# Layer 3 of a four-layer image network: the depthwise convolution of image b done by VectorE, and both engines' instruction orders written by hand

## The chip, the cores and the metric

The kernel runs on one core of a Trainium2 chip. The metric is the device time of one execution, in microseconds (us). A core has several engines that run side by side, each with its own queue of instructions taken in order: TensorE (PE) multiplies matrices and writes only to PSUM, the accumulator memory; VectorE (DVE) does elementwise work; ScalarE (ACT) does copies and functions such as Gelu; GpSimd (POOL) does small elementwise work; SyncE (SP) issues transfers between the core's working memory (SBUF) and the device memory. Engines wait for one another through semaphores.

## The reference

The input x is 4 images of 48 channels and 256 x 256 pixels, fp32. Four layers follow, each of the form x = x + f(normalised x), where the normalisation is over 16 groups of channels. Layer 0 is a gated convolution block, layers 1 and 2 are scans over rows and columns, and layer 3, which the change is about, is this:

```
y  = einsum(w_in, x)                    # 48 -> 288 channels
f  = rfft2(8x8 patches of y) * mask     # a weight per channel and frequency
y  = irfft2(f)
y  = depthwise 3x3 convolution(y, w_dw) # each channel with its own nine taps
x1, x2 = halves of y                    # 144 channels each
out = einsum(w_out, gelu(x1) * x2)      # 144 -> 48 channels
```

## The kernel before, in words

**Steps.** Layer 3 (`layer3`, from L707) takes the images two at a time: image a and image b of a pair. A pair is worked through in 32 steps of 8 rows and a short last step, so there are 66 steps, 64 of them full. A convolution needs one row above and below, so each step keeps ten rows and copies two of them from the step before.

**Tiles of a step.** Of the 288 channels of an image, 144 are x1 and 144 are x2. The first 128 of x1 are one tile, the first 128 of x2 another: a0 and a1 for image a, b0 and b1 for image b. The remaining 16 + 16 channels of both images share a fifth tile, m, of 64 partitions.

**Pieces.** Each step is prepared by pieces of TensorE work, each with its evacuation: `normed` (ScalarE normalises the fetched rows into u), `turned` (TensorE transposes u, 16 columns of pixels at a time; ScalarE copies), `waves` (the forward transform of the patches, into xf), `spectrum` (per column of 8 x 16 pixels the product with w_in into PSUM, L841, and the mask multiplied onto it by VectorE into z, L843 and L847), `pixels` (the inverse transform of one of the five tiles, L872, copied by ScalarE, L876, into the tile zt; GpSimd copies the two old rows, L865).

**The convolution.** `taps` (L883) does it on TensorE: one tap of a channel is a product with a diagonal matrix. It uses 32 x 32 tiles of the array; two *lanes* of work, lane 0 on the partitions 0 to 63 and lane 1 on 64 to 127, each put one tap at a time, 8 matmuls of 512 pixels, into the order. Lane by lane the sums of the first and second half are gathered in PSUM; `gate` (L896) takes Gelu of the first on ScalarE (L903) and multiplies it with the second on VectorE (L904). The layer has four PSUM buffers of two banks each, which is all of PSUM, and every piece and every running sum takes one.

**The store.** `mixed` (L906) multiplies the gated channels with w_out (L917): 32 partitions at a time, image a into the PSUM partitions 0 to 63 and image b into 64 to 127. It takes two PSUM buffers. VectorE adds the layer's input (L930), SyncE stores.

**The order.** `in_turns` (L427) writes TensorE's order by hand: in each round both lanes put one tap each if they can, a tap earns `pace` of credit, and pieces are put in as long as there is credit for their charge. A piece can have a condition (the last user of its tile is through); a lane waits until its tile is ready. The list of pieces is `work` (L965). Only TensorE's order is fixed (L721); the instructions of VectorE, ScalarE, GpSimd and SyncE are ordered by the framework's planner, which goes by its own costs. PSUM and SBUF buffers are handed out by the planner too. Layer 0 uses the same `in_turns`.

Of the kernel before, what the change touches and what calls it, by code (L numbers as in the profile page):

```python
# [15 lines left out]
C = 48  # L16
# [3 lines left out]
PW = 16  # L20
# [8 lines left out]
class Net:  # L29
# [396 lines left out]

    def in_turns(self, lanes, pieces, pace):  # L427


        piece, credit, count = next(pieces), 0.0, 0  # L430
        while lanes or piece:
            moved = 0
            for k, l in enumerate(list(lanes)):
                if k == 1 and count < 4:
                    continue
                got = next(l, None)
                if got is None:
                    lanes.remove(l)
                moved += bool(got)
            count += moved > 0  # L440
            credit = min(credit + pace * moved, 2.0)
            while piece and piece[0]() and (credit >= 0 or not moved):
                piece[2]()
                credit, moved = credit - piece[1], 1
                piece = next(pieces, None)
            assert moved or not lanes

# [259 lines left out]
    def layer3(self, x, scs):  # L707
# [9 lines left out]
        with ExitStack() as st:  # L717
            pool = lambda name, bufs, **k: st.enter_context(tc.tile_pool(name=name, bufs=bufs, **k))
            wp, io, mid = pool("w3", 1), pool("io3", 2), pool("mid3", 1)
            ps_w = pool("ps3w", 4, space=PSUM)  # L720
            st.enter_context(tc.manual_schedule(engines={mybir.EngineType.PE}))  # L721

# [25 lines left out]
            for k in range(3):  # L748
                for t in range(9):
                    nc.vector.tensor_scalar(diag[:, k, t, :], eye, wd[:, k, t : t + 1], None, ALU.mult)  # L750


            wo = wp.tile([128, 6, 64], F32, name="wo")
            nc.gpsimd.memset(wo, 0.0)
            for j in range(4):
                s = slice(32 * j, 32 * j + 32)
                nc.sync.dma_start(
                    wo[s, 0:4, 0:C], self.a["L3_w_out"][0:NM, :].rearrange("(k c) o -> c k o", c=32)
                )
                for b in range(2):  # L760
                    at = 32 * j + NR * b
                    nc.sync.dma_start(wo[at : at + NR, 4 + b, 0:C], self.a["L3_w_out"][NM:HD, :])
# [13 lines left out]
            for p in range(self.NP):  # L776
# [4 lines left out]
                scp.append(t)  # L781
            gated = {g: wp.tile([128, 4, MM], F32, name=f"g_{g}", tag=f"g_{g}") for g in "ab"}
            gated["m"] = wp.tile([128, 1, MM], F32, name="g_m", tag="g_m")
# [15 lines left out]
            def normed(step):  # L799
                raw, sc = raw_of[step], scp[step[0]]  # L800
                u = mid.tile([112, NQ, 2, RB, PW // 2], F32, name="u")
                for e in range(2):
                    for l in range(2):
                        nc.scalar.activation(
                            u[:, l::2, e].rearrange("p v h w -> p v (h w)"),
                            raw[0:112, e, :, :, l * 8 : l * 8 + 8].rearrange("p (v f) h w -> p v (f h) w", f=2),
                            AF.Identity, bias=sc[0:112, 1:2], scale=sc[0:112, 0:1],
                        )
                return u
# [15 lines left out]
            def waves(xt):  # L825
                xf = mid.tile([112, NQ, 128], F32, name="xf")
                for q0 in range(0, NQ, 8):
                    pf = ps_w.tile([128, 8, 128], F32, name="pf", tag="w")
                    for q in range(8):
                        nc.tensor.matmul(pf[0:112, q, :], xt[:, q0 + q, :], self.dft_p, start=True, stop=True)  # L830
                    nc.scalar.copy(xf[:, q0 : q0 + 8, :], pf[0:112])
                return xf
# [63 lines left out]
            def gate(step, img, k0, x1, x2):  # L896
# [7 lines left out]
                nc.vector.tensor_tensor(to[0:n, k0:k1, 0:m], gl[0:n, 0 : k1 - k0, 0:m], flat(x2), ALU.mult)  # L904

            def mixed(step):  # L906

                p, s = step
                h0 = s * RB - 1
                js, n = (range(1), 1) if tail(step) else (range(4), R2)  # L910
                pos = [ps_w.tile([128, 2, R2, W], F32, name="po", tag="w") for _ in js[::2]]
                for i in range(5):
                    for j in js:
                        for b in range(2):
                            r = slice(32 * j, 32 * j + 32)
                            src = gated["m"][r, 0] if i == 4 else gated["ab"[b]][r, i]
                            nc.tensor.matmul(  # L917
                                pos[j // 2][64 * b : 64 * b + 64, j % 2, 0:n, :], wo[r, i + b * (i == 4), :],
                                src[:, 0 : n * W].rearrange("p (r w) -> p r w", w=W),
                                start=(i == 0), stop=(i == 4),  # L920
                            )
# [24 lines left out]
            def lane(l):  # L946

                for n, step in enumerate(steps):
                    for img in ("a", "b") + (("m",) if step[1] % 2 == l else ()):
                        pds = []  # L950
# [14 lines left out]
            def work():  # L965
# [3 lines left out]
                def back(step, k):  # L969
# [5 lines left out]

                    free = lambda: last not in steps or k == 4 or taken.get((last, order[k]), 0) == 2
                    return free, 0.0 if tail(step) else 3.8, go

# [6 lines left out]
                def front(step):  # L985
                    yield always, 1.8, lambda: state.update(xt=turned(state["u"]))
                    yield always, 3.8, lambda: state.update(xf=waves(state["xt"]))

                def spectra():
                    for q in range(0, NQ, 2):  # L990
                        yield always, 1.2, both(*[lambda q=q + i: spectrum(state["xf"], q) for i in range(2)])

                def store(step):
                    full = lambda: all(taken.get((step, g), 0) == (1 if g == "m" else 2) for g in order)

# [3 lines left out]

                    return full, 4.5, go  # L1000

                fetch(steps[0])
                state["u"] = normed(steps[0])
                yield from front(steps[0])
                yield from spectra()
                fetch(steps[1])
                yield back(steps[0], 0)
                yield back(steps[0], 1)
                for n, step in enumerate(steps):
                    nxt = steps[n + 1] if n + 1 < len(steps) else None  # L1010
                    ahead = nxt is not None and not tail(nxt)
                    later = steps[n + 2] if n + 2 < len(steps) else None
                    if ahead:
                        state["u"] = normed(nxt)
                    yield back(step, 2)
                    if n:
                        yield store(steps[n - 1])
                    if later is not None and not tail(later):
                        fetch(later)
                    yield back(step, 3)  # L1020
                    if ahead:
                        yield from front(nxt)
                    yield back(step, 4)
                    if ahead:
                        yield from spectra()
                    if nxt is not None:
                        yield back(nxt, 0)
                        yield back(nxt, 1)
                yield store(steps[-1])

            self.in_turns([lane(0), lane(1)], work(), 0.6)


# [104 lines left out]
```

## Time and profile before

| what | value |
|---|---|
| time, median of 3 runs | 14801.05 us (14797.25 to 14808.69) |
| time of the profiled execution | 14797.92 us |
| its span, first to last instruction | 14796.1 us |
| layer 3, from its first transposes to the end | 9342 to 14796 us |
| TensorE matmuls busy in the span | 94% |
| VectorE, ScalarE, GpSimd busy | 33%, 20%, 10% |
| in 12800 to 13800 us (layer 3): TensorE, VectorE, ScalarE, GpSimd | 995.7, 246.1, 263.2, 29.5 us of 1000 |

The profile is of one execution. Its slices cut the span into 40 equal parts, with a digit for the tenths that an engine was busy. A row of the groups of instructions gives line, engine, operation, tiles (out<-in), shape and count, then busy time in us and mean ns of one, then the idle time of that engine just ahead of these instructions and what ended it. A row of the timeline gives start and length in us, and merges like instructions. An fp32 matmul is recorded twice, so counts of matmul records are twice those in the code. The ends of matmuls are modelled, and neighbours overlap; the distance from start to start is what counts. Some matmul records are missing.

### The profile page before, as it was taken

The page shows a single profiled execution, that of the slowest core. Times are in us where ns is not written, and L with a number is a line of the kernel's source. Part 1 is how long each engine was busy: PE and PEld are TensorE (multiplying, and loading weights), DVE is VectorE, ACT ScalarE, POOL GpSimd, SP SyncE. Part 2 cuts the span into 40 slices and gives each one's busy share as a digit, 9 for nine tenths or more (in the row PEclk, how much of TensorE's full clock was granted, in tenths as well). Part 3 has the DMA queues.
Part 4 walks back from the last instruction along what each step waited for, and adds up shares of the span by engine and source line. Part 5 has one row for each costly group of instructions (what it writes and reads, how often), then busy time and mean ns, then how long its engine had stood idle before and what let it go on. Part 6 is the DMA issues. An engine that isn't in the chain of part 4 may idle for free.

```text
span 14796.1 us, 417160 instructions
## 1 busy us (share of the span) xinstructions
PE 13940.6 (94%) x194676; PEld 8922.0 (60%) x194676; DVE 4880.6 (33%) x11213; ACT 3022.1 (20%) x2916; POOL 1429.3 (10%) x1225
## 2 busy tenths in 40 slices
PE   3999999998999898889999988899999999999999
PEld 1444444445777676667776766555665666666666
DVE  5333333333333334433333344322222222222222
ACT  1222222222223000012330000222222222222222
POOL 0000000000000004410000144000000000000000
PEclk9999999999999999999999998999999999999999
DMA  7222222114755876777568677211111111111110
GB/s 162 49 48 51 47 49 52 47 45 92 154 133 161 160 150 162 176 148 152 138 157 158 141 172 178 34 24 20 20 24 20 20 22 22 20 24 20 21 23 18
DMA packets 1168959, 1224.08 MB, mean 83 GB/s; under 512 B 1025796, under 2 KB 1030396, under 8 KB 1106364
## 3 DMA queue, kind: packets, MB, share of 16 engines
q1 hardware_dynamic: 1069116, 649.60, 23.0%
q0 software_dynamic: 87488, 445.55, 10.8%
q10 hardware_dynamic: 10624, 102.24, 3.4%
q8 instruction: 1527, 25.02, 0.7%
q14 instruction: 204, 1.67, 0.0%
HBM read 699.82 MB, written 497.42 MB: 81 GB/s over the span
## 4 chain that ended last, share of the span: by engine, by line
PE 89%; DMA 6%; DVE 1%; SPq 1%; issue 1%; POOL 1%; ACT 0%; ACTq 0%; DVEq 0%; POOLq 0%
PE acc L493 32%; PE pd L889 19%; PE pd L270 13%; PE pp L872 8%; PE pz L841 4%; PE ph L245 3%; DMA blk<-x 3%; PE po L917 2%; PE pf L830 2%; PE po L355 2%; PE pf L333 1%; PE py L302 1%; DMA x<-blk 1%; DMA gx<-in_x 1%; POOL blk L686 1%
## 5 line engine op out<-in xcount | busy, mean ns | idle before, releaser
L493 PE MATMUL acc<-line,w_down 96*96 96x256 f32 x12240 | 2650.7, 379 | 41.8 <-DMA in<-x 23.2
L493 PEld LDWEIGHTS acc<-line,w_down 96*96 96x96 f32 x12240 | 1996.1, 163 | 695.7 <-issue 42.5
L270 PE MATMUL pd<-main,diag 32*32 32x512 f32 x36864 | 1671.3, 599 | 25.3 <-issue 25.0
L889 PE MATMUL pd<-z_a,diag 32*32 32x512 f32 x37152 | 1672.1, 596 | 5.8 <-DVE g_m L904 5.3
L889 PE MATMUL pd<-z_b,diag 32*32 32x512 f32 x37152 | 1651.0, 596 | 14.0 <-DVE g_a L904 13.1
L493 PE MATMUL acc<-line,w_left 96*96 96x256 f32 x6120 | 1359.4, 385 | 252.0 <-DVE line L676 252.0
L493 PE MATMUL acc<-line,w_right 96*96 96x256 f32 x6120 | 1338.9, 381 | 103.4 <-DVE line L637 38.9
L493 PEld LDWEIGHTS acc<-line,w_left 96*96 96x96 f32 x6120 | 1015.4, 166 | 595.7 <-DVE line L676 258.0
L872 PEld LDWEIGHTS pp<-c_idft,z 128*128 128x128 f32 x10240 | 1156.9, 181 | 288.7 <-issue 187.0
L493 PEld LDWEIGHTS acc<-line,w_right 96*96 96x96 f32 x6120 | 1004.2, 164 | 438.1 <-DVE line L637 40.9
L872 PE MATMUL pp<-c_idft,z 128*128 128x128 f32 x10240 | 1224.1, 278 | 19.3 <-ACT z_b L876 18.7
L843 DVE TENSOR_TENSOR z<-pz,mask 128x512 f32<-128x512 f32 x1024 | 702.8, 686 | 1427.6 <-PE pz L841 1427.6
L270 PEld LDWEIGHTS pd<-main,diag 32*32 32x32 f32 x36864 | 594.4, 103 | 649.0 <-issue 528.4
L270 PE MATMUL pd<-rest,diag 32*32 32x512 f32 x18432 | 938.0, 597 | 25.2 <-issue 25.2
L889 PEld LDWEIGHTS pd<-z_a,diag 32*32 32x32 f32 x37152 | 639.4, 103 | 491.1 <-issue 305.6
L889 PEld LDWEIGHTS pd<-z_b,diag 32*32 32x32 f32 x37152 | 593.2, 103 | 489.4 <-issue 304.1
L686 POOL TENSOR_TENSOR blk<-blk,line 96x1024 f32<-96x1024 f32 x248 | 705.8, 2874 | 864.8 <-DVE line L676 445.8
L637 DVE SCALAR_TENSOR_TENSOR line<-acc,b_right,in 96x256 f32<-96x256 f32 x1020 | 488.7, 479 | 884.6 <-PE acc L493 838.4
L596 DVE SCALAR_TENSOR_TENSOR line<-acc,b_down,in 96x256 f32<-96x256 f32 x992 | 475.6, 479 | 809.1 <-PE acc L493 809.1
L556 DVE TENSOR_TENSOR line<-acc,in 96x256 f32<-96x256 f32 x1020 | 429.0, 421 | 927.7 <-PE acc L493 912.9
L102 ACT ACTIVATE nrm<-nrm 96x2 f32<-96x2 f32 (+1 forms) x4 | 0.8, 204 | 3339.4 <-DVE nrm L101 3339.4
L603 ACT COPY blk<-line 96x1024 f32<-96x1024 f32 (+2 forms) x264 | 482.0, 1889 | 935.7 <-DVE line L596 755.9
(138 smaller groups left out, 12057.3 us busy)
## 6 DMA issues: line engine op xcount, KB each, us to landing
blk<-x ACTq DMA_DIRECT2D x64, 1536.0 KB, 23.3
in<-x SPq DMA_DIRECT2D x248, 384.0 KB, 10.9
dn<-line POOLq DMA_DIRECT2D x124, 768.0 KB, 9.3
rt<-line POOLq DMA_DIRECT2D x124, 768.0 KB, 10.1
in<-rt SPq DMA_DIRECT2D x124, 768.0 KB, 7.3
in<-dn SPq DMA_DIRECT2D x120, 768.0 KB, 5.7
in<-up SPq DMA_DIRECT2D x240, 384.0 KB, 11.2
up<-blk POOLq DMA_DIRECT2D x56, 1536.0 KB, 23.8
```

The lines of the kernel that those rows point to most:

```text
L245: nc.tensor.matmul(ph[to, b, 0 : r1 - r0, :], wi[s, at : at + m], xn[s, r0:r1, :], start=True, stop=True)
L270: nc.tensor.matmul(pd[32 * j : 32 * j + 32, i], diag[s, img // 2, t, :], z[s, R2 * j + t // 3 : R2 * j + t // 3 + R2, t % 3 : t % 3 + W], ...
L493: self.nc.tensor.matmul(acc, w[:, t, :], carry[:, :, t : t + m], start=(t == 0), stop=(t == 2))
L556: nc.vector.tensor_tensor(blocks(inner(line)), blocks(acc), xin[p][:, :, r % 2, :, r // 2, :], ALU.add)
L596: nc.vector.scalar_tensor_tensor(inner(line), acc, bd, new[p][r], ALU.add, ALU.add)
L603: nc.scalar.copy(blk[p][:, :, e, lo:hi, k // 2 : k // 2 + RH], inner(ln[p][:, e::2])[..., lo:hi].rearrange("p h i w -> p i w h"),)
L637: nc.vector.scalar_tensor_tensor(blocks(inner(line)), blocks(acc), br, new, ALU.add, ALU.add)
L686: (nc.vector if w0 == 0 else nc.gpsimd).tensor_tensor(part, part, inner(ln[p][:, f::2])[..., lo:hi].rearrange("p w i h -> p i h w"), ALU.add)
L841: nc.tensor.matmul(pz[:, b, 0 : 2 * HD], xf[s, q, :], wi[s, :], start=True, stop=True)
L843: nc.vector.tensor_tensor(z[:, q, 0 : 2 * n].rearrange("p (b c) -> p b c", b=2), pz[:, :, 0:n], mask[:, :, 0:n].to_broadcast([128, 2, n]), ...
L872: nc.tensor.matmul(pp[0:n, q // 4, :, q % 4 * PW : (q % 4 + 1) * PW], z[:, q0 + q, k * NM : k * NM + n], self.idft, start=True, stop=True,)
L889: nc.tensor.matmul(pd[32 * j : 32 * j + 32, i, 0:n, :], diag[s, 2 if g == "m" else half, t, :], zt[g][s, R2 * j + t // 3 : R2 * j + t // 3 ...
```

## The change

- Image b's tiles b0 and b1 are no longer convolved by `taps`. A new generator `side` does it for the whole tile: ScalarE does the first tap (Identity with the tap's weight as scale) into an accumulator in SBUF, VectorE adds the other eight with `scalar_tensor_tensor`, four rows (1024 elements) at a time; ScalarE takes Gelu of b0's accumulator, VectorE multiplies the two. Image b's gates and its buffer `g_b` go.
- VectorE's order is fixed by hand too. `in_turns` keeps a second account: each round adds TensorE's charge of that round, less what VectorE has to do for the pieces (a fourth entry of a piece), and `side` puts in its instructions as long as that account is positive.
- The store multiplies image b's product as a whole: one matmul of 128 partitions for each pair of rows, ahead of image a's; image a's and the remainder's are as before. It now also waits for `side`.
- The lanes take the remainder m before image a, and the list of pieces is turned: spectrum, b0, turn, b1, wave, m, store of the step before, a0, a1. Charges and pace are new. A debt of credit is cut at 5.
- u and xf share one SBUF buffer. One more weight tile and a column of zeros are set up before the first step.

```diff
-    def in_turns(self, lanes, pieces, pace):
+    def in_turns(self, lanes, pieces, pace, side=iter(())):
-        piece, credit, count = next(pieces), 0.0, 0
+        piece, credit, count, ahead, cost = next(pieces), 0.0, 0, 0.0, 1.0
...
+            spent += 0.54 * moved
             credit = min(credit + pace * moved, 2.0)
             while piece and piece[0]() and (credit >= 0 or not moved):
                 piece[2]()
-                credit, moved = credit - piece[1], 1
+                credit = max(credit - piece[1], -5.0)
+                moved, spent = 1, spent + piece[1] - sum(piece[3:])
                 piece = next(pieces, None)
+            ahead = max(min(ahead + spent, 4.0), -4.0)
+            while ahead > 0 or not moved:
+                cost = next(side, None)
+                if not cost:
+                    break
+                ahead, moved = ahead - cost, 1
...
-            st.enter_context(tc.manual_schedule(engines={mybir.EngineType.PE}))
+            st.enter_context(tc.manual_schedule(engines={mybir.EngineType.PE, mybir.EngineType.DVE}))
...
+            def side():
+                for step in steps:
+                    rows = 1 if tail(step) else RB
+                    sums = []
+                    for half in range(2):
+                        g = f"b{half}"
+                        while (step, g) not in ready:
+                            yield 0.0
+                        acc = mid.tile([128, RB, W], F32, name=f"acc{half}", tag=f"acc{half}", bufs=2 - half)
+                        sums.append(acc)
+                        for t in range(9):
+                            for r in range(0, rows, RB // 2):
+                                r1 = min(rows, r + RB // 2)
+                                z = zt[g][:, r + t // 3 : r1 + t // 3, t % 3 : t % 3 + W]
+                                w = wd[:, half, t : t + 1]
+                                if t == 0:
+                                    nc.scalar.activation(acc[:, r:r1], z, AF.Identity, bias=none, scale=w)
+                                    continue
+                                nc.vector.scalar_tensor_tensor(acc[:, r:r1], z, w, acc[:, r:r1], ALU.mult, ALU.add)
+                                yield 0.05 + 0.28 * (r1 - r)
+                        taken[step, g] = 2
+                        if half == 0:
+                            nc.scalar.activation(acc[:, 0:rows], acc[:, 0:rows], AF.Gelu)
+                    for r in range(0, rows, RB // 2):
+                        r1 = min(rows, r + RB // 2)
+                        nc.vector.tensor_tensor(sums[0][:, r:r1], sums[0][:, r:r1], sums[1][:, r:r1], ALU.mult)
+                        yield 0.05 + 0.28 * (r1 - r)
+                    whole[step] = sums[0]
...
+                part = whole.pop(step)
+                for j in js:
+                    nc.tensor.matmul(
+                        pos[j // 2][64:128, j % 2, 0:n, :], wo_b, part[:, R2 * j : R2 * j + n, :],
+                        start=True, stop=False,
+                    )
                 for i in range(5):
                     for j in js:
-                        for b in range(2):
+                        for b in range(2) if i == 4 else range(1):
...
-                                start=(i == 0), stop=(i == 4),
+                                start=(b == 0 and i == 0), stop=(i == 4),
...
-                    for img in ("a", "b") + (("m",) if step[1] % 2 == l else ()):
+                    for img in (("m",) if step[1] % 2 == l else ()) + ("a",):
...
-                        yield always, 1.2, both(*[lambda q=q + i: spectrum(state["xf"], q) for i in range(2)])
+                        yield always, 2.2, both(*[lambda q=q + i: spectrum(state["xf"], q) for i in range(2)]), 2.1
...
-                    return full, 4.5, go
+                    return full, 8.2, go, 3.5
...
+                    if not tail(step):
+                        yield from spectra()
+                    yield back(step, 2)
                     if ahead:
                         state["u"] = normed(nxt)
-                    yield back(step, 2)
+                        turn, wave = front(nxt)
+                        yield turn
+                    yield back(step, 3)
+                    if ahead:
+                        yield wave
+                    yield back(step, 4)
                     if n:
                         yield store(steps[n - 1])
                     if later is not None and not tail(later):
                         fetch(later)
-                    yield back(step, 3)
...
+                    yield back(step, 0)
+                    yield back(step, 1)
                 yield store(steps[-1])
-            self.in_turns([lane(0), lane(1)], work(), 0.6)
+            self.in_turns([lane(0), lane(1)], work(), 1.12, side())
```

## The prediction

> **What bounds the kernel now.** I read first the slices of the page, to see which engine fills which part of the span.
>
> ```profile
> PE   3999999998999898889999988899999999999999
> DVE  5333333333333334433333344322222222222222
> PEclk9999999999999999999999998999999999999999
> ```
>
> Layer 3 is the right part: its first transposes stand at 9342 us, so it has 14796 - 9340 = 5456 us of the span. TensorE is full there at full clock, VectorE is two tenths busy. Second, the groups of instructions of that stretch, by shape.
>
> ```profile
> L889 PE MATMUL pd<-z_b,diag 32*32 32x512 f32 x36795 | 1626.2, 598 | 13.9 <-DVE g_a L904 13.1
> L843 DVE TENSOR_TENSOR z<-pz,mask 128x512 f32<-128x512 f32 x1008 | 691.7, 686 | 1401.2 <-PE pz L841 1401.2
> L904 DVE TENSOR_TENSOR g_b<-gl,pd 128x1024 f32<-128x1024 f32 x128 | 153.4, 1220 | 1353.1 <-PE pd L889 1349.6 <-ACT gl L903 3.4
> L930 DVE TENSOR_TENSOR xo<-po,raw 112x256 f32<-112x256 f32 x512 | 175.8, 418 | 311.7 <-PE po L917 284.1 <-issue 27.6
> ```
>
> Read the last column: VectorE's idle time ends on TensorE everywhere, while TensorE loses 14 us on image b's taps in the whole layer. Third, the timeline of TensorE, for prices by distance from start to start (a matmul leaves two records).
>
> ```profile
> 9438.52 1.24 PE L841 MATMUL pz<-wi,xf 48*128 48x288 f32 x8
> 9439.69 1.95 PE L889 MATMUL pd<-z_m,diag 32*32 32x512 f32 x32
> 9441.56 1.24 PE L841 MATMUL pz<-wi,xf 48*128 48x288 f32 x8
> ...
> 11044.00 1.14 PE L889 MATMUL pd<-z_b,diag 32*32 32x512 f32 x32
> 11045.07 3.84 PE L872 MATMUL pp<-c_idft,z 128*128 128x128 f32 x32
> 11048.84 3.43 PE L889 MATMUL pd<-z_b,diag 32*32 32x512 f32 x96
> ```
>
> Two taps, one of each lane (32 records), take 1.07 us; two of one lane alone (9439.69 to 9441.56) take 1.87. Two spectrum columns (pz) take 1.17, an inverse transform (pp) 3.77. Fourth, VectorE's timeline at the store, for the length of a step.
>
> ```profile
> 9478.23 2.41 DVE L930 TENSOR_TENSOR xo<-po,raw 112x256 f32<-112x256 f32 x7 [27.62 <-issue]
> ...
> 12214.59 2.41 DVE L930 TENSOR_TENSOR xo<-po,raw 112x256 f32<-112x256 f32 x7 [4.87 <-PE po L917]
> ...
> 14770.48 2.74 DVE L930 TENSOR_TENSOR xo<-po,raw 112x256 f32<-112x256 f32 x8 [3.85 <-PE po L917]
> ```
>
> The first and third rows are step 0 of the first pair and step 31 of the second; with 12214.59 (step 0 of the second) and 12075.00 (step 31 of the first, same view) there are 31 intervals of 83.8 us and 31 of 82.4: **83.1 us a step**.
>
> **What the Trainium skill says.** "VectorE: DVE Perf Modes", section on the TRN2 errata: an fp32 tensor_tensor takes (N+151)/0.96 ns, 1224 ns for 1024 elements; the trace agrees (L904: 1220). Its table of perf modes gives two-tensor fp32 operations one element a cycle in SBUF too; no row of this trace shows that for contiguous rows. "SBUF — State Buffer", Who interferes with whom: a VectorE instruction with two SBUF inputs contends with a GpSimd instruction that reads SBUF; not shown before. "TensorEngine Tiling (Array Packing)", Key Properties: separate tiles work in parallel; the 1.07 against 1.87 above is that. "ScalarE: Activation LUTs", What ACT_TABLE_LOAD costs: 280 ns + 0.833 ns an element, 93 ns more for a second pointer operand; L804's 807 ns for 512 agrees, so a first tap of 1024 is an estimated 1.23 us.
>
> **TensorE's sum.** Removed: image b's 36 lane taps of a step, 18 pairs x 1.07 = 19.3. Added at the store: image a's and b's products ran beside each other, 4.7 us for 80 records (11081.65 to 11086.29), and each of eight tiles took one record in 0.43. Image a alone keeps eight records on each of its tiles, 3.4; b's four full-height products are eight records on one tile, 3.4; the remainder 0.9 and the start 0.4 stay: 8.1, so +3.4. Moved: the remainder's nine taps now come before image a. Walking the turn rule with its charges by hand, some six of them find the other lane blocked: 6 x (0.94 - 0.53) = +2.4. The old wait for the remainder's gate just before the store (1.4 us in the chain of waits) goes, since that gate now comes a step early. 83.1 - 19.3 + 3.4 + 2.4 - 1.4 = **68.2 us**.
>
> **VectorE's sum.** Added: 32 multiply-adds and 2 products of 1024 elements. Two gates in a row take 2.35 us (L904), so one after another costs 1.13; the pointer scalar costs 0.06 alone (L637 479 against L556 421). I take 1.16; 1.07 (elements alone) and 1.28 (no overlap) bound it: 34 x 1.16 = 39.4. Kept: spectrum 16 x 0.73, gates 2.3 + 0.6, store 2.7 = 17.3; b's gates (2.3) go. 57 us, below 68: engine totals leave TensorE the bound, and what remains is order.
>
> **The order of a step**, by the same walk. Phase A: eight spectrum pieces with a pair of taps each, 8 x (1.17 + 1.07) = 17.9, where VectorE has 11.7 of spectrum and no multiply-adds. Phase B on TensorE: b0's inverse transform, turn, b1's, wave, m's with taps between, gate of lane 0 after 23.0 us, five taps, store at 26.0, five solo taps, a0's and a1's inverse transforms.
>
> On VectorE, b0's first multiply-add waits for the end of b0's transform (3.8), the last copy (1.03), ScalarE's first tap (1.23) and handovers of 0.1: 6.3 us into B. Twenty multiply-adds are written before lane 0's gate: it starts at 6.3 + 20 x 1.16 = 29.5, 30 with a halo copy of GpSimd (0.61) in the way, and ends at 31.2. The store needs two of the four PSUM buffers; at 26 two are held by image a's second halves and one by m. So its second half waits for that gate, which before was prompt. Store end: 31.2 + 1.7 (two b products) + 3.4 + 0.9 + handovers = 37.6 instead of 34.1: **3.5 us lost**. Next late: the output additions, behind which twelve side operations and the next spectrum stand on VectorE. They start at 37.7; 2.7 + 12 x 1.16 + 0.6 brings VectorE to 55.0, while TensorE (4.7 solo, 2 x 3.77, four pairs 4.3) comes to phase A at 54.0. Two free buffers cover most of it: 0.3 lost. Step: 68.2 + 3.5 + 0.3 = **72.0 us**.
>
> **At no cost**, with their cover: ScalarE gains four first taps (4.7) and about as much Gelu as it loses, some 27 us of 72; if its queue put the Gelu of b's sum before a PSUM copy, TensorE would wait (counted below). POOL's halo copies for b now wait for VectorE instead of TensorE, a phase ahead of need. u and xf share memory: the normalising (2.9 us on ScalarE) runs after the last spectrum matmul, under b0's transform (3.8); without that cover 2 us a step. SP's stores and fetches keep their place after the store; two memsets and one small DMA are added before the first step. Layer 0 passes through the same turn rule, where only a debt beyond five units is cut: its first three pieces, 5.4.
>
> **Sum.** 83.1 - 72.0 = 11.1 us for each of 63 intervals = 699, and about 20 for the first step, in which a, b and m ran one after another: 720. Own time 14797.9 - 720 = 14078; the median stands 3 higher: **14080 us**.
>
> **Rivals.** *TensorE alone sets the step*: the gate is prompt because multiply-adds cost 1.07 or the buffers fall well. Step 68.2, saving 14.9 x 63 + 20: **13840**. For it: 57 against 68 in total. Against it: the written order puts 20 multiply-adds ahead of a gate that TensorE reaches at 23.
>
> *The store waits for both gates*: if the planner hands the store the two buffers held by image a, it starts at 31.2 and its second half waits for lane 1's gate (34.9): +3.3; or ScalarE's queue costs as much. Step 75.3, saving 491 + 20: **14290**. For it: the planner places ScalarE and buffers by its own costs. Against it: TensorE's small waits before (14 us on that line).
>
> *Slower*: VectorE's operations with both inputs in SBUF. The only such row is strided:
>
> ```profile
> L686 DVE TENSOR_TENSOR blk<-blk,line 96x960 f32<-96x960 f32 x8 | 13.7, 1777 | 0.0
> ```
>
> With its small form (254 ns for 64) that is 1.70 ns an element, 1.79 us for 1024 instead of 1.16. All 32 stand on the path above: +20 us, step 92, **15350**. It decides from 1.16 + 11.1 / 32 = 1.51 us on. Against it: these rows are contiguous, and the skill's price is 1.04 ns an element.
>
> That image b stays on TensorE can't be: no matmul reads its tiles but the store's.
>
> **How the numbers follow.** The forecast (step 71 to 73.5: 13990 to 14170) 0.46, TensorE alone 0.20, both gates late 0.22, something between that and no gain (79 us and more) 0.03, slower 0.08, a draw 0.01. Range: 13860 leaves out the best of the second case; 14340 takes in the third and a multiply-add of 1.28 (+0.12 x 32 x 63 = 242). About 0.2% can be told from no change; faster 0.91, same 0.01, slower 0.08.
>
> **What would show it.** Right: no matmuls on z_b; multiply-adds 1.13 to 1.20 apart; store pieces near 8.1 us of work with a wait on VectorE's gate between; 72 us from store to store; VectorE 75 to 80% busy in layer 3, idle ahead of the output additions and of b0's first tap. Wrong: a multiply-add beyond 1.5 us, TensorE waiting in phase A for the spectrum or on ScalarE's copies, solo taps at 1.07, or a layer 0 of other length than 3510 us.

## The result, and the profile after

The changed kernel takes 14867.93 us (median of 4 runs, 14860.04 to 14874.17) against 14799.74 us for the kernel before: a ratio of 1.0044, with an interval of 1.0029 to 1.0059. It is slower by about 0.4%. The forecast was 14080 us, 5% faster, with a range that ended at 14340. It is wrong in sign and by 788 us. The profiled execution took 14874.17 us, its span 14872.4.

The slices of the changed kernel's page, to be read as those of before:

```profile
PE   3999999998999898889999978788888888888888
DVE  5333333333333334433333445666666666666666
PEclk9999999999999999999999988899999989999999
```

Layer 3 is again the right part; it starts within a few us of where it did. TensorE has lost a tenth (it was at nine), VectorE has gone from two to six. The layers before it are unchanged. Next come two groups of layer 3 by shape, then VectorE's output additions in the timeline (step 0 of each pair and step 31 of the second):

```profile
L943 DVE SCALAR_TENSOR_TENSOR acc<-z_b,wd,acc 128x1024 f32<-128x1024 f32 x2048 | 2465.5, 1276 | 395.3 <-ACT acc L941 395.3
L857 DVE TENSOR_TENSOR z<-pz,mask 128x512 f32<-128x512 f32 x1024 | 702.3, 686 | 590.3 <-PE pz L855 588.6
```

```profile
9471.37 2.41 DVE L984 TENSOR_TENSOR xo<-po,raw 112x256 f32<-112x256 f32 x7 [6.06 <-PE po L971]
12256.65 2.41 DVE L984 TENSOR_TENSOR xo<-po,raw 112x256 f32<-112x256 f32 x7 [6.21 <-PE po L971]
14854.87 2.74 DVE L984 TENSOR_TENSOR xo<-po,raw 112x256 f32<-112x256 f32 x8 [6.77 <-PE po L971]
```

With step 31 of the first pair at 12109.96, there are 31 intervals of 85.1 us and 31 of 83.8: 84.5 us a step by the measure that gave 83.1 before, where 72.0 was predicted. 12.5 x 62 = 775 is nearly the whole error. So the question is where 12.5 us a step went. The multiply-adds did not eat them: each is busy for 1276 ns, but 18 in a row take 21.61 us from first start to last end, one every 1.20, where 1.16 was taken and 1.28 was the upper bound.

The chain of waits through the middle of one step, then the waits of layer 3 (9500 to 14872 us: engine, line, what it waited for; us in total, times, longest):

```profile
11004.27 1.29 DVE acc L943
...
11005.59 1.91 ACT acc L947
11007.50 0.91 ACT xf L845
...
11008.45 5.58 PE pp L886 x32
```

```profile
PE pp L886 <- ACT xf L845: 552.3, 59, 9.4
PE pd L903 <- DVE g_m L918: 93.1, 30, 4.8
PE pp L886 <- DVE g_m L918: 57.7, 31, 2.2
```

A multiply-add is followed by the Gelu of b's sum (L947), that by the copy of the forward transform out of PSUM (xf, L845), and only then m's inverse transform runs. TensorE waits 9.4 us for this in nearly every step. ScalarE's timeline has both in one queue:

```profile
11005.59 1.91 ACT L947 ACTIVATE acc<-acc 128x2048 f32<-128x2048 f32 x1 [10.07 <-DVE acc L943]
11007.41 1.91 ACT L845 COPY xf<-pf 112x1024 f32<-112x1024 f32 x2
```

The planner, which still orders ScalarE, put the Gelu ahead of the two copies. It needs b0's sixteenth multiply-add; the copies were ready long before, and stand behind it for 10 us. The other two waits are for m's gate, which VectorE does behind eleven multiply-adds and two products; the prediction did not have them.

What follows a wait is dearer than the wait. In TensorE's timeline after a wait of 2.44 us:

```profile
10869.33 3.95 PE L903 MATMUL pd<-z_a,diag 32*32 32x512 f32 x48 [2.44 <-DVE g_m L918]
10873.21 2.29 PE L855 MATMUL pz<-wi,xf 48*128 48x288 f32 x8
10875.43 2.01 PE L903 MATMUL pd<-z_a,diag 32*32 32x512 f32 x32
10877.37 2.13 PE L855 MATMUL pz<-wi,xf 48*128 48x288 f32 x8
10879.42 1.14 PE L903 MATMUL pd<-z_a,diag 32*32 32x512 f32 x32
10880.50 1.24 PE L855 MATMUL pz<-wi,xf 48*128 48x288 f32 x8
```

For 10 us after it two spectrum columns take 2.22 us instead of 1.17 and a pair of taps 1.94 instead of 1.07: half speed. The m transform above shows the same, 5.58 us where it takes 3.71 in other steps and kernels. The Trainium skill ("TensorE: Matmul & The Clock Gate", What's actually happening) describes this: the clock is halved when TensorE has been idle over a window of about 3.4 us, and given back after as long a busy one. Here a wait of 2.44 us, shorter than that window, was enough, and the return took 10; the third experiment below has waits of the same length without any loss of clock. The mean clock granted in layer 3 is 0.92, where before it was 1.00.

### The profile page after: what moved, and what is told of

The parts are those of the page before. It is cut to its first block, busy times and chain, and to the rows that moved or that the text cites. A ratio compares the mean times of both kernels' runs of the same rounds, so it can differ in the third digit from the quotient of the medians.

```text
span 14872.4 us, 340743 instructions
## 1 busy us (share of the span) xinstructions
PE 13297.2 (89%) x155976; PEld 8329.4 (56%) x155976; DVE 7342.2 (49%) x13291; ACT 3320.0 (22%) x3110; POOL 2818.1 (19%) x1227
## 4 chain that ended last, share of the span: by engine, by line
PE 73%; DVE 15%; DMA 6%; ACT 2%; issue 2%; SPq 1%; POOL 1%; ACTq 0%; DVEq 0%; POOLq 0%
PE acc L502 32%; PE pd L270 13%; DVE acc L943 13%; PE pd L903 7%; PE pp L886 5%; PE pz L855 4%; PE ph L245 3%; DMA blk<-x 3%; PE po L971 2%; PE po L355 2%; PE po L962 2%; DMA x<-blk 1%; PE pf L333 1%; PE py L302 1%; DMA gx<-in_x 1%
## 5 line engine op out<-in xcount | busy, mean ns | idle before, releaser
L943 DVE SCALAR_TENSOR_TENSOR acc<-z_b,wd,acc 128x1024 f32<-128x1024 f32 (+1 forms) x2080 | 2481.1, 1264 | 396.6 <-ACT acc L941 395.3
L879 POOL COPY z_b<-z_b 128x512 f32<-128x512 f32 x128 | 1470.2, 11486 | 3096.1 <-DVE acc L943 3053.8
L886 PE MATMUL pp<-c_idft,z 128*128 128x128 f32 x10240 | 1374.7, 298 | 645.4 <-ACT xf L845 558.8
L886 PEld LDWEIGHTS pp<-c_idft,z 128*128 128x128 f32 x10240 | 1304.4, 194 | 925.9 <-ACT xf L845 613.4
L903 PE MATMUL pd<-z_a,diag 32*32 32x512 f32 x37152 | 1589.0, 619 | 105.9 <-DVE g_m L918 93.9
L502 PE MATMUL acc<-line,w_right 96*96 96x256 f32 x6120 | 1335.1, 380 | 104.9 <-DVE line L646 40.9
L903 PEld LDWEIGHTS pd<-z_a,diag 32*32 32x32 f32 x37152 | 415.1, 105 | 622.3 <-issue 352.4
L685 DVE SCALAR_TENSOR_TENSOR line<-acc,b_left,in 96x256 f32<-96x256 f32 x992 | 475.7, 480 | 529.8 <-PE acc L502 529.8
```

Of the source, the lines that this page charges most:

```text
L502: self.nc.tensor.matmul(acc, w[:, t, :], carry[:, :, t : t + m], start=(t == 0), stop=(t == 2))
L685: nc.vector.scalar_tensor_tensor(inner(line), acc, bl, new[p][r], ALU.add, ALU.add)
L879: nc.gpsimd.tensor_copy(t[:, 0:2, 1 : W + 1], above[:, RB : RB + 2, 1 : W + 1])
L886: nc.tensor.matmul(pp[0:n, q // 4, :, q % 4 * PW : (q % 4 + 1) * PW], z[:, q0 + q, k * NM : k * NM + n], self.idft, start=True, stop=True,)
L903: nc.tensor.matmul(pd[32 * j : 32 * j + 32, i, 0:n, :], diag[s, 2 if g == "m" else half, t, :], zt[g][s, R2 * j + t // 3 : R2 * j + t // 3 ...
L943: nc.vector.scalar_tensor_tensor(acc[:, r:r1], z, w, acc[:, r:r1], ALU.mult, ALU.add)
```

## The experiments

There were three theories at the start. **Q**, ScalarE's queue: the Gelu of b's sum stands ahead of the xf copies, and without that the step is near the prediction. **V**, VectorE's length: its chain of multiply-adds, gates and additions sets the step, and a wait taken away comes back elsewhere. **K**, the clock: it is low for a reason of its own and not because of the waits. All kernels are the changed kernel with an edit. The kernel before, run beside them on the same chips, took 14791 to 14799 us.

### 1. No Gelu of b

```diff
-                        if half == 0:
-                            nc.scalar.activation(acc[:, 0:rows], acc[:, 0:rows], AF.Gelu)
```

> Leaves out ScalarE's Gelu of image b's sum; all else is the change. Theory Q (ScalarE's queue): in the changed kernel this Gelu stands ahead of the two copies of the forward transform (xf) and waits for the 16th multiply-add of b0, so TensorE waits 9.4 us a step and its clock then halves for about 2 us. Without it the waits of TensorE on xf vanish (under 0.5 us a step), the step falls from 86 to 74.5 to 78 us and the time to 14130 to 14350. Theory V (VectorE's own length, 34 operations at 1.20 us and what they hold back, sets the step, and the wait on xf is only where it shows): the wait moves to another line and the time stays at 14750 or more. Theory K (the clock alone): as Q for the time, but the granted clock in layer 3 would have to stay near 0.92 while the time stays high.

14499.52 us, one run; span 14497.7. This leaves out Gelu for image b. The wait on xf is gone, and the time falls by 368 us, 5.8 us a step. Q is right in kind, V's number (14750 and more) is not met, but the saving is well short of the 518 to 738 us that Q had expected. What the wait had hidden is now seen, in the waits of this kernel (9500 to 14400 us):

```profile
PE po L960 <- DVE g_a L918: 188.4, 59, 4.9
PE pd L903 <- DVE g_m L918: 93.3, 30, 4.8
PE pp L886 <- DVE g_m L918: 56.2, 30, 2.2
```

The first row is the wait that the prediction had reckoned with: the store's second PSUM buffer waits for lane 0's gate. It is 3.2 us a step, 3.5 was predicted. In the changed kernel TensorE came so late to the store that the gate was done.

### 2. The Gelu put later, nothing left out

```diff
-                        for t in range(9):
+            early = [(0, t) for t in range(8)]
+            late = [(1, t) for t in range(5)] + [(0, 8)] + [(1, t) for t in range(5, 9)]
...
+                        for h, t in late if half else early:
...
+                            if (h, t) == (0, 8):
+                                nc.scalar.activation(acc[:, 0:rows], acc[:, 0:rows], AF.Gelu)
```

> The whole computation: the last tap of b0 is put off until after tap 4 of b1, behind the output additions of the store on VectorE, and the Gelu of b with it, so that ScalarE's queue holds it behind the copies of xf and of m. Theory Q: as without the Gelu, with at most 2 us a step lost on image a's copies, which now stand behind it: 14130 to 14450, a ratio to the kernel before of 0.955 to 0.976. Theory V: 14750 or more, no faster than before by more than 0.5%.

14505.2 us (14500.13 to 14558.24), ratio 0.9813, interval 0.9792 to 0.9833. b0's last tap and the Gelu come after tap 4 of b1. This is faster than both kernels, and still outside Q's range, which ended at 14450: Q is not the whole of it. A step is 78.8 us by the measure above (79.25 and 78.28), so the Gelu's place was worth 84.5 - 78.8 = 5.7 us. VectorE's and TensorE's timelines at the store, where b0's inverse transform began at 11026.12:

```profile
11032.40 24.01 DVE L946 SCALAR_TENSOR_TENSOR acc<-z_b,wd,acc 128x1024 f32<-128x1024 f32 x20 [6.17 <-ACT acc L944]
11056.32 1.21 DVE L918 TENSOR_TENSOR g_a<-gl,pd 128x1024 f32<-128x1024 f32 x1
```

```profile
11051.91 1.93 PE L966 MATMUL po<-acc,wo_b 128*64 128x512 f32 x4
11057.59 3.67 PE L966 MATMUL po<-acc,wo_b 128*64 128x512 f32 x4 [3.75 <-DVE g_a L918]
```

The prediction's walk through this phase is there nearly to the tenth: first multiply-add 6.3 us in (predicted 6.3), lane 0's gate at 30.2 behind 20 multiply-adds (30), the store at 25.8 (26), a wait of 3.75 us (3.5). What it did not have is in the second row of TensorE: after the wait the same four products take 3.67 us instead of 1.93.

### 3. Eight of image b's nine taps left out

```diff
-                        for t in range(9):
+                        for t in range(1):
```

> Leaves out the eight VectorE taps of each of b's tiles (the first tap on ScalarE, Gelu and product stay), so TensorE's work and order of pieces are those of the change and VectorE has 19 us a step. It measures TensorE's sum of the prediction: step 68.2, time 13840; 13800 to 13950 if the sum is right. If TensorE's work was mis-sized (solo taps, the store of 8.1 us), the time is 14000 or more.

14050.32 us, one run. The convolution of b is cut to its first tap, so VectorE is nearly as idle as before the change. The expectation for a right sum of TensorE's work was 13800 to 13950, and this is outside it. A step is 71.6 us. But TensorE waits here for the copies of the transposes (xt), which the other kernels hardly show (0.5 us): with the multiply-adds gone the Gelu of b's sum comes early, and stands ahead of these copies in ScalarE's queue. The waits, ScalarE's rows, and TensorE's row in two steps:

```profile
PE pp L886 <- ACT xt L834: 143.5, 59, 2.4
```

```profile
11030.96 1.91 ACT L947 ACTIVATE acc<-acc 128x2048 f32<-128x2048 f32 x1
11032.77 1.69 ACT L834 COPY xt<-pt 128x896 f32<-128x896 f32 x2
```

```profile
11033.71 5.47 PE L886 MATMUL pp<-c_idft,z 128*128 128x128 f32 x32 [2.43 <-ACT xt L834]
11106.98 3.84 PE L886 MATMUL pp<-c_idft,z 128*128 128x128 f32 x32 [2.43 <-ACT xt L834]
```

Without that wait the step is 69.2 us. The two rows of TensorE are the same work after the same wait, once at half speed and once not; the clock records of this trace have half speed after 22 of the 59 waits, an estimated 0.6 us a step. So TensorE's sum, 68.2 us, was off by about half a us, and 72 us was within its reach. Most of the 12.5 us is not TensorE's work.

### 4. VectorE's order given back to the planner

```diff
-            st.enter_context(tc.manual_schedule(engines={mybir.EngineType.PE, mybir.EngineType.DVE}))
+            st.enter_context(tc.manual_schedule(engines={mybir.EngineType.PE}))
```

> The change with VectorE's order left to the planner. In its order the gates of image a stand behind 26 to 30 multiply-adds instead of 20, and the output additions behind all of them; the Gelu stays ahead of the copies of xf. Theory Q: the wait on xf stays at about 9 us a step, the store comes later by 7 to 10 us in addition, and the time is 14850 to 15300. Theory V, by which the hand order of VectorE costs through its waits ahead of the output additions (6.5 us a step): faster than the change, 14500 or less.

14910.35 us, one run. The wait on xf stays at 9.4 us, and the store waits for the gates of image a besides (139.5 and 56.0 us in all). This is in the range of Q (14850 to 15300). Fixing VectorE's order by hand is not what costs: in this one run the planner's order is no faster, 42 us slower.

### 5. Fewer multiply-adds ahead of the gates, and the output additions apart

After the second run the open theory was **G**: what is left over 72 us is the waits on VectorE's two gates and the half clock behind them. Two edits of the written order were made on top of the later Gelu, one by one and together. The first lets `side` start later, the second makes the output additions a piece of their own, so that some multiply-adds can stand between the gates and them.

```diff
                         while (step, g) not in ready:
                             yield 0.0
+                        if half == 0:
+                            yield 5.0
```

```diff
-                    return full, 8.2, go, 3.5
+                    yield full, 4.1, go, -4.1
+                    yield always, 4.1, lambda: added(step, state["pos"]), 7.6
```

> Whole computation; the later Gelu of the run before stays, and side() starts some five cost units later, so about 16 multiply-adds instead of 20 are written before image a's gates. Theory G (in phase B the store waits 3.75 us for lane 0's gate on VectorE, and TensorE then runs its products at half clock, some 1.8 us more): gate at 6.3 + 16 x 1.2 = 25.5 instead of 30, so both go: step 73 to 75 instead of 79.2, total 14130 to 14260. Theory V (VectorE's chain as a whole sets the step, multiply-adds moved back return as waits elsewhere): 14430 or more, with TensorE waiting for the spectrum or for the product of b.

> Whole computation; the later Gelu stays, and the store's output additions are a piece of their own, some five multiply-adds after the matmuls. 21 multiply-adds stay ahead of image a's gates. Theory G: the store's wait stays at about 3.75 us, gate m comes earlier by nothing, so 14450 to 14550, as the later Gelu alone (14505). Theory V: the additions no longer hold the multiply-adds up, so VectorE's chain shortens by the wait for the store (2 to 4 us a step): 14260 to 14380.

> Whole computation; both edits on top of the later Gelu: the later start of side() and the output additions apart. 16 to 17 multiply-adds before image a's gates, gate m ahead of image a's first inverse transform. Theory G: store wait and the wait for gate m (1.6 to 2.7 us in most steps, with half clock behind it) both go; what is left is TensorE's 72 us: step 72 to 74, 14060 to 14180. Theory V: 14430 or more; four to six VectorE operations of b spill into phase A, and TensorE waits there for the spectrum's PSUM buffers.

- Later start: 14409.27 us, ratio 0.9743 (0.9727 to 0.9759). Both theories' numbers failed (14130 to 14260 was G's, 14430 and more V's). The wait for lane 0's gate is gone, as G said. A new one has its place: 283.1 us in 55 places on image a's copies, because the Gelu of b's sum now stands ahead of *these* in ScalarE's queue. It is the fault of the first run over again at another place:

```profile
10632.85 1.91 ACT L953 ACTIVATE acc<-acc 128x2048 f32<-128x2048 f32 x1 [20.68 <-DVE acc L948]
10634.66 1.93 ACT L890 COPY z_a<-pp 128x1024 f32<-128x1024 f32 x2
```

- Additions apart: 14598.35 us, one run; slower than the second run by 93. G had expected no change (14450 to 14550), V a gain. With other turns of the lanes, TensorE needs image a's buffer before m's taps, and waits in the first pair 8.87 us for a gate that still stands behind 20 multiply-adds: 83.7 us a step, and 76.7 in the second pair, which has no such wait there.
- Both: 14356.29 us, ratio 0.9705 (0.969 to 0.9719). G had expected 14060 to 14180, V 14430 and more: neither.

The third is the telling one, for its two pairs of images differ. Their written orders are not the same, as the turns of the lanes fall differently. In the first pair m's taps stand directly behind m's transform and need a buffer of image a; in the second a pair of image a's taps is in between, and this wait does not show. TensorE's row of the first pair, then the busy times, with the granted clock in the last column but two, for a stretch of each pair:

```profile
11052.46 4.94 PE L903 MATMUL pd<-z_m,diag 32*32 32x512 f32 x48 [4.09 <-DVE g_a L918]
```

```profile
9500.00:11800.00 2300.00, 2165.19 (x29631) 1136.30 (x29637) 1692.93 (x2181) 746.06 (x762) 141.92 (x113) 0.94 0.11 21
12250.00:14200.00 1950.00, 1892.96 (x27552) 1044.60 (x27521) 1547.46 (x2017) 701.48 (x715) 302.04 (x105) 1.00 0.12 23
```

With the wait, 79.96 us a step and a clock of 0.94; without it, in the same execution, 73.3 us and 1.00. The difference is 6.7 us with a wait of 4.09. The second pair has waits of its own that the first has not (1.2 us on image a's copies, 0.5 on the transposes'), so an estimated 4 us of the difference is slower work behind the long wait: b's products after it take 4.86 us here, 3.65 in the second pair. This speaks against K.

### 6. Hold the multiply-adds until the gates are written

Shifting by charges moves everything a little. So the next edit says outright what is wanted: after its thirteenth multiply-add `side` stops until both gates of image a have been written.

```diff
+                                while done == 13 and n and passed.get(steps[n - 1], 0) < 2:
+                                    yield 0.0
+                                done += 1
                                 nc.vector.scalar_tensor_tensor(acc[:, r:r1], z, w, acc[:, r:r1], ALU.mult, ALU.add)
...
                             gate(step, img, 2 * l, *pds)
+                            passed[step] = passed.get(step, 0) + 1
```

> Whole computation; side() starts as in the changed kernel again, the output additions stay apart and Gelu stays late, but side() holds after its thirteenth multiply-add until both gates of image a are written. Theory G: lane 0's gate starts at 6.3 + 13 x 1.24 = 22.4 after b0's inverse transform begins, before TensorE needs its buffer at 23.3, in both pairs; so the 4.1 us wait of the first pair and its half clock (80.9 us a step against 74.2) go: 73.5 to 76 us in both pairs, total 14120 to 14260, clock 0.99 to 1.00 in layer 3. Theory K (the clock is low in the first pair whatever the waits): first pair stays above 78 us, total 14300 or more.

> Whole computation; as the run before, and b0's last tap and its Gelu are put after tap 6 of b1, so in ScalarE's queue the Gelu stands behind the Gelu of m's gate and the first of image a's copies. Theory G: 0 to 1.2 us a step less than the run before (what TensorE still waits for image a's copies): total 14060 to 14200. If the Gelu's place no longer matters: equal to the run before within 20 us.

14166.33 us (ratio 0.9578, 0.9563 to 0.9592) with the Gelu as in the second run, 14088.74 us (0.9522, 0.9506 to 0.9538) with the Gelu two taps later still. Both lie in G's ranges. The first pair of images, where m's taps still stand directly behind m's transform, falls from 79.96 to 72.9 us a step in the first of these kernels, with a clock of 1.00 instead of 0.94; K had it stay above 78. The difference between the two kernels, 78 us, is 1.2 us a step, at the upper end of what was expected. It includes TensorE's wait on image a's copies, 54.7 us in 30 places, which the second kernel doesn't show.

### 7. The hold with the Gelu in its first place, and the hold alone

**O** is the theory that the gates' place in VectorE's order also decides ScalarE's order, so that the Gelu needs no edit. The first kernel keeps the hold and the additions apart, and has the changed kernel's own sequence of taps and Gelu:

```diff
-            early = [(0, t) for t in range(8)]
-            late = [(1, t) for t in range(5)] + [(0, 8)] + [(1, t) for t in range(5, 9)]
+            early = [(0, t) for t in range(9)]
+            late = [(1, t) for t in range(9)]
```

The second is the changed kernel with the hold and nothing else.

> Whole computation; the run with the gates first and the additions apart, but with the taps of b and the Gelu in the changed kernel's own sequence. In ScalarE's written order the Gelu now stands behind the copies of xf and m all the same, since it follows the gates. Theory O (the place of the gates in VectorE's order decides ScalarE's order too; the Gelu needs no edit of its own): no wait on xf, 14090 to 14180, no worse than 15 us above the better of the two runs before. Theory Q (the Gelu's own place is a cost apart): at least 4 us a step, 14340 or more.

> Whole computation; the changed kernel with the hold alone: side() stops at its thirteenth multiply-add until both gates of image a are written; store and Gelu as in the changed kernel. On VectorE the gates are followed by the output additions at once, so VectorE stands idle from about 24.7 us after b0's transform begins to the store's end at 33, and some six multiply-adds go over into the spectrum: 76 to 79 us a step, 14250 to 14450. If splitting the additions off was worth nothing: 14080 to 14180.

14083.39 us (14075.61 to 14094.95), ratio 0.9519, interval 0.9504 to 0.9533, and 14329.34 us (0.9682, 0.9665 to 0.9698), in the range expected. O holds, with a time 7 us under its range; in the second kernel too, which has the hold alone, TensorE's wait on xf is gone. ScalarE's and TensorE's rows of the first of them, in a step whose b0 transform began at 10603.55:

```profile
10620.98 1.01 ACT L845 COPY xf<-pf 112x1024 f32<-112x1024 f32 x1 [0.41 <-PE pf L844]
...
10632.06 1.91 ACT L954 ACTIVATE acc<-acc 128x2048 f32<-128x2048 f32 x1 [3.50 <-DVE acc L949]
```

```profile
10627.36 3.40 PE L903 MATMUL pd<-z_m,diag 32*32 32x512 f32 x48 [0.50 <-DVE g_a L918]
10630.69 3.65 PE L969 MATMUL po<-acc,wo_b 128*64 128x512 f32 x8
```

The Gelu is now behind both xf copies, by the planner's own choice, since its last multiply-add is written after the gates. The store runs at full clock. All that TensorE waits for in 9500 to 14000 us is 56 us; the step is 72.6 us in the first pair and 72.1 in the second. The busy times of a stretch of the first pair (length, TensorE, its weight loads, VectorE, ScalarE, GpSimd, then the clock):

```profile
9500.00:11900.00 2400.00, 2360.95 (x34002) 1300.23 (x34001) 1927.62 (x2499) 865.61 (x884) 172.87 (x139) 1.00 0.12 23
```

TensorE is full at full clock, VectorE 80% busy (75 to 80% was predicted). All of VectorE's work is done in this step, so V is wrong. The hold alone gives 538 us of the 784 us from the changed kernel to this one; its step is 76.1 us, and it still waits for m's gate (96.3 and 29.1 us). With the hold in place, the additions apart and the charges that go with them give the other 246, 3.8 us a step.

## Why the prediction was wrong

**What held.** The bound (TensorE, with VectorE's total below it) and its sum: 68.2 us against 69.2 in the third experiment, an estimated 68.6 without the half speed there. (One term of it was read too large: m's old gate before the store, 1.4 us in the chain of waits, left TensorE idle for 0.55 us, at 11081.65 of the kernel before.) VectorE's price: 1.16 us against 1.20. The first multiply-add, the gate behind 20 multiply-adds and the store's wait on it, as seen in the second. Layer 0 has the slices it had. Nothing of SyncE's queue shows in the waits of TensorE. The kernel with the hold and the additions apart, which has all of the change's parts in it, takes 72.35 us a step and 14083 us in all. That is the predicted time, but by luck, for it is another kernel and not the predicted step: the store's 3.5 us are gone from it, and the spectrum takes 20.0 us instead of 17.9, with two multiply-adds and two products written into it (18.1 in the third experiment, without them).

**The step that failed** is the paragraph "At no cost", in its sentence on ScalarE: "if its queue put the Gelu of b's sum before a PSUM copy, TensorE would wait (counted below)". It was counted in half a clause of the second rival, "or ScalarE's queue costs as much", at 3.3 us that belonged to another wait. Both orders written by hand were walked through; ScalarE's, which nobody writes, was covered by its total of 27 us out of 72. Yet the Gelu could not start before the sixteenth multiply-add, 6.3 + 16 x 1.2 = 25.5 us after b0's transform began, and the first xf copy behind it is done 1.91 + 0.95 us later, at 28.4. In the changed kernel TensorE comes to m's transform at 19.0 (10999.07 after 10980.05). The wait, if the Gelu stood first, could be had from such numbers: 28.4 - 19.0 = 9.4 us, which is what the chain shows. This term was 3.3 and should have been 9.4, with its clock, and far more than the 0.22 that it shared was due. Taking the wait away gave back 5.7 to 5.8 us a step, as it had covered others (first and second experiments); the two points that follow are part of the other 6.8 of the 12.5, which were not split up to the last us.

**A wait was priced at its own length.** Every wait of the prediction (3.5, 3.3, 0.3) was taken as time lost and no more. The runs show slower work behind a wait: 1.74 us in the first four products after a wait of 3.75 in the second experiment, an estimated 4 after 4.09 in the fifth, nothing or 1.63 after 2.4 in the third. In the second experiment the mean clock from 9500 to 14000 us is 0.95. That is one part of why it ends at 78.8 us, with the predicted wait in it, and not at 72.0, and of why the second rival's 14290 was not the worst of its kind.

**m's gate was left out.** It frees the PSUM buffer that image a's transform or its first solo taps need. The prediction put twelve side operations ahead of the spectrum and asked who waits for the spectrum; m's gate stood among the same operations, at 0.6 us, without anyone that waits for it. The waits of the changed kernel for it are 150.8 us in 61 places, 2.5 us each; in the second experiment they are 104.9 us in 53 places from 9500 to 14000 us.

**Rivals.** The slower case was right in sign for a reason that wasn't there: 1.51 us a multiply-add was its threshold, 1.20 was measured. A slower outcome by queues, with two such waits in a step, was not among the cases; it should have been the slower one.

**What stays open.** Why the planner put the Gelu first was not tried beyond the fact that the written place of the gates turns it round. What decides whether half clock follows a wait, and for how long, was not measured by itself, and the length is not enough: waits of 2.4 us brought it in 22 of 59 cases in the third experiment, and in the changed kernel one of them brought it for 10 us. The buffers were handed out by the planner in every run, so what another choice of buffers would do is not known.

## What to carry to other kernels

When work moves to an engine whose order is planned or hand-written, walk through the queue of every engine that shares a buffer with it, also of the one with idle time: a single instruction with a late input holds up everything behind it. Write the instructions that free another engine's buffers (gates, evacuations) first, and fill in the long work behind them; here that one rule, given as a hold of thirteen, turned a loss of 0.4% into a gain of 3.2%, and with the additions moved apart 4.8%. Price a wait of TensorE of 2 us or more above its length: here 2.4 us cost from 2.4 to an estimated 6.9 us with the slower work behind it, and 4.09 us about twice its length.

## What the runs showed of the hardware

**GpSimd beside VectorE.** The group of GpSimd's copies of two old rows in the changed kernel:

```profile
L879 POOL COPY z_b<-z_b 128x512 f32<-128x512 f32 x128 | 1470.2, 11486 | 3096.1 <-DVE acc L943 3053.8
```

It took 613 ns before and takes 11,486 now, beside VectorE's unbroken run of multiply-adds. The Trainium skill ("SBUF — State Buffer", Who interferes with whom) says that the two engines lock each other out of a shared port when VectorE has two inputs in SBUF; the trace agrees for GpSimd and shows no loss for VectorE, whose multiply-adds keep their 1.20 us. A copy stands until VectorE's run is over:

```profile
10997.34 13.47 POOL L879 COPY z_b<-z_b 128x512 f32<-128x512 f32 x1 [27.94 <-DVE acc L943]
```

It ends at 11010.81; VectorE's run of multiply-adds ends at 11010.34. TensorE doesn't wait for these copies here. In the kernel with the hold and the additions apart their mean is 2442 ns in 9500 to 14000 us, and there VectorE pays: one copy starts at 10621.20 and takes 1.52 us, and the multiply-add beside it takes 1.62 us instead of 1.27. Why the copies get in earlier there was not tried.

**Half clock after short waits.** Waits of 2.44, 3.75 and 4.09 us on TensorE were each followed by matmuls at half speed in the steps shown above, in one case for 10 us; waits of 0.5 us were not. The length of the wait doesn't decide it alone, as the two rows of the third experiment show. In the clock records of the changed kernel's layer 3, 94 of the 96 stretches at half speed last 3.4, 6.8 or 10.2 us, and 69 of them 10.2.
